# Deformable convolution beside its own set-up: the first batch's places in two halves, and the norm's scales of later batches spread by DMA

## Chip, cores and metric

The kernel runs on one core of a Trainium2 chip. The metric is device time in microseconds for one execution of the whole program; lower is better.

## What is computed

The program is a network of four layers over `x` of 4 batches, 128 channels and 64 x 64 places. Each layer adds a token mixer over a channel norm, and then a feed-forward part. The change lies in the mixer of the second layer, a modulated deformable 3 x 3 convolution. Cut to what matters:

```python
x = x + _L1_conv_ref(_ln_c(x), w_off, b_off, w_mod, b_mod, weight, bias)

def _ln_c(v, eps=1e-6):                     # over the channels of each place
    m = mean(v, axis=1); s = var(v, axis=1)
    return (v - m) / sqrt(s + eps)

def _deform_forward(x, ...):                # K = 3, PAD = 1
    off = conv2d(x, w_off, b_off)           # dy, dx of each place and tap
    mask = sigmoid(conv2d(x, w_mod, b_mod))
    py, px = place + tap + dy, place + tap + dx
    y0, x0 = floor(py), floor(px);  ly, lx = py - y0, px - x0
    # four neighbours, zero outside the image
    sampled = v00*(1-ly)*(1-lx) + v01*(1-ly)*lx + v10*ly*(1-lx) + v11*ly*lx
    return einsum('bckhw,ock->bohw', sampled * mask, weight) + bias
```

## The kernel before

The image stays in SBUF as `xs` (128 channels by 4 batches of 4096 places). The phases run one after another; the deformable stage follows a recurrence and comes before an expert-choice layer.

**The set-up of a batch** is the generator `plan(b)`. Eight chunks of 512 places are centred by a matmul (`centred`), squared on ACT and summed on PE (`deviations`). The root's reciprocal is taken on DVE (`inverted`), in two halves of four chunks. `scaled` spreads one row of the reciprocals over the 128 partitions with a matmul against a broadcast column of the identity, into PSUM, and multiplies the centred chunk by it on DVE (L792, L801). `turned` transposes a chunk by rows and writes it to a table in DRAM, pairs of neighbouring rows side by side (PE L818, ACT L820 and L812, SP L827 and, for the last chunk, L829); its PSUM bank has the tag "pt" (two banks) for batch 0 and "pd" (one bank) for the others, and its SBUF tile `dcn_xt` has two buffers. `offsets` is the small 3 x 3 convolution, four chunks to a call, 36 matmuls, four transposes and four copies into `off` (L840, L849, L853, L858). `places` turns all offsets of the batch, 32 tiles of 128 places by 9 taps, into indices `idx` and weights `w` on DVE and ACT (L915 to L978); L944 writes the indices.

**The main loop** walks over batches, chunks of 512 places (`c`, 8 of them) and 7 of the 9 taps. For each tap it takes four tiles of 128 places in two pairs. `taken` issues two gathers from the table (L998, one indirect DMA a tile, on POOL's queue) into one of eight buffers `dcn_g`, and multiplies them on DVE by their weights, which are held in PSUM (L1006). Two steps later `joined` transposes and adds them on PE (L1015, eight to a pair), then ACT copies (L1120) and `convolve` multiplies by the tap's weights (L1127). The other two taps, the middle column's, are made from hat functions instead of gathers (`hats`, `fold`, L1030 to L1062).

**The order** on PE, ACT, DVE and POOL is the order in which the program is written; SP's DMAs are placed by a scheduler. One `step()` follows each pair: it runs what is due from earlier steps, takes one item of the generator `side` (every fifth step one more), and one item of `hats`. `side` is `plan(b + 1)`. What is left of it at the head of the next batch is drained in one go:

```python
for b in range(B):
    for _ in side:
        pass
    side = plan(b + 1) if b + 1 < B else iter(())
```

`plan(0)` has nothing to run beside and is issued whole ahead of the loop. Its second part sets `turned` of the last four chunks abreast of `offsets(0)`, `offsets(1)` and `places`. `keep` stores `idx` and `w` for a fallback, which is taken only where an offset is over 2.

Of the kernel before, what the change touches and what calls it, by code (L numbers as in the profile page):

```python
# [7 lines left out]

# [2 lines left out]

# [17 lines left out]
P = 128  # L29
# [563 lines left out]
class Sampling:  # L593
# [8 lines left out]
    def __init__(self, net, one, dram):  # L602
# [4 lines left out]
        self.all_idx = [dram.tile([NCH, P, 4 * KK], I32, name=f"dcn_all_idx{b}") for b in range(B)]  # L607
        self.all_w = [dram.tile([NCH, P, 16 * KK], F32, name=f"dcn_all_w{b}") for b in range(B)]
        self.tables = [dram.tile([SIDE * SIDE + 1, 2, P], F32, name=f"dcn_table{b}") for b in range(B)]
        zero = one.tile([SIDE + 1, 2 * P], F32, name="dcn_zero")  # L610
        nc.gpsimd.memset(zero, 0.0)

# [82 lines left out]
def deformable(net, sampling):  # L695
# [19 lines left out]
    with ExitStack() as ctx:  # L715
# [2 lines left out]
        ps = ctx.enter_context(tc.tile_pool(name="dcn_ps", bufs=2, space=PSUM))  # L718
        (xp,) = padded_pair(net, one, PAD, "dcn_pad", 1)
        cw = one.tile([P, NH * P], F32, name="dcn_cw", bufs=1)  # L720
        far = one.tile([P, B + 1], F32, name="dcn_far")
        beyond = one.tile([1, 2], F32, name="dcn_beyond")
        rowts = []
        for i in range(2):
# [11 lines left out]
        def plan(b):  # L736
# [1 line left out]

            def bank(tag="pd" if b else "pt"):
                return ps.tile([P, CH], F32, name=f"dcn_{tag}", tag=tag, bufs=BANKS[tag])

            def inside(c):
# [29 lines left out]
            def inverted(h):  # L774
# [11 lines left out]
                )  # L786
                yield

            def scaled(c):
                rows = slice(32 * (c % 4), 32 * (c % 4) + 32)  # L790
                pb = bank()
                nc.tensor.matmul(  # L792
                    pb,
                    net.ident[rows, rows.start : rows.start + 1].to_broadcast([32, P]),
                    rstds[c // 4][rows],
                    start=True,
                    stop=True,
                )
                yield
                d = inside(c)  # L800
                nc.vector.tensor_mul(d, d, as_shape(pb, d))  # L801
                yield

            xts = []
# [70 lines left out]
                    yield  # L875

            yield from inverted(0)
            for c in half:
                yield from scaled(c)
            if b == 0:  # L880
                yield from abreast(
                    one_by_one(*(turned(c) for c in half)),
                    one_by_one(inverted(1), *(scaled(4 + c) for c in half)),
                )
                yield from abreast(
                    one_by_one(*(turned(4 + c) for c in half)),
                    one_by_one(offsets(0), offsets(1), places(b, off)),
                )
                return
            yield from turned(0)  # L890
            yield from turned(1)
            yield from inverted(1)
            yield from turned(2)
            yield from turned(3)
            for c in half:
                yield from scaled(4 + c)
            yield from offsets(0)
            yield from turned(4)
            yield from turned(5)
            yield from offsets(1)  # L900
            yield from turned(6)
            yield from turned(7)
            yield from places(b, off)

        def places(b, off):

            frac, row = [], new("row")
            hat = sb.tile([P, NT, NH, PICKED], F32, name="dcn_hat", tag="dcn_hat", bufs=1)
            apart = sb.tile([P, NT, NH, 1], F32, name="dcn_apart", tag="dcn_apart", bufs=1)
            pieces = sb.tile([P, NT, NH * PICKED, 3], BF16, name="dcn_pieces", tag="dcn_pieces")  # L910
            at = slice(H0, H0 + NH)
            for axis in range(2):
                pos, low, lowi, over = new("pos"), new("low"), new("lowi", I32), new("over")
                frac.append(new(f"frac{axis}"))
                nc.vector.tensor_add(pos, grids[axis], off[:, :, axis : 18 : 2])  # L915
                if axis == 0:
                    nc.vector.tensor_sub(apart[:, :, :, 0], pos[:, :, at], grids[0][:, :, at])
                    yield
                    nc.vector.tensor_reduce(
                        far[:, b : b + 1],  # L920
                        apart.rearrange("p t k o -> p (t k o)"),
                        AX.X,
                        ALU.max,
                        apply_absolute_value=True,
                    )
# [12 lines left out]
                if axis == 0:  # L938
                    nc.vector.tensor_scalar(row, low, float(SIDE), float(SIDE + 1), op0=ALU.mult, op1=ALU.add)
                else:  # L940
                    nc.vector.tensor_add(row, row, low)
                yield
            idx = new("idx", I32)
            nc.vector.tensor_copy(idx, row)  # L944
            ly, lx = frac
            mask, lo, hi = new("pos"), new("low"), new("over")
            w = new("w")
            wq = [w[:, :, :, q] for q in range(4)]
            nc.scalar.activation(mask, off[:, :, 18:27], AF.Sigmoid)
            yield  # L950
            rows_of = hat[:, :, :, 1:]
            shape = [P, NT, NH, PICKED - 1]
            nc.vector.tensor_tensor(
                rows_of, apart.to_broadcast(shape), sampling.steps[:, :, :, 1:].to_broadcast(shape), ALU.add
            )
            nc.scalar.activation(rows_of, rows_of, AF.Abs)
            yield
            nc.scalar.activation(rows_of, rows_of, AF.Relu, bias=sampling.ones, scale=-1.0)
            nc.vector.tensor_mul(rows_of, rows_of, mask[:, :, at].unsqueeze(3).to_broadcast(shape))
            yield  # L960
            left = hat.rearrange("p t k j -> p t (k j)")
            for a in range(3):
                nc.vector.tensor_copy(pieces[:, :, :, a], left)
                if a < 2:
# [12 lines left out]
            nc.vector.tensor_mul(wq[0], lo, lx)  # L977
            nc.vector.tensor_mul(wq[1], hi, lx)  # L978
            made[b] = (sampling.squares(tables[b]), idx, w, pieces, turns[b])
            yield  # L980

# [121 lines left out]
        with tc.manual_schedule(engines=ORDERED):  # L1103
# [44 lines left out]
            for b in range(B):  # L1148
                for _ in side:
                    pass  # L1150
                side = plan(b + 1) if b + 1 < B else iter(())
                rows, idx, w, pieces, turned = made.pop(b)
                for more in busy:
                    for _ in more:
# [2 lines left out]
                for tile in range(5):  # L1157
                    fold(b, tile, turned)
                for c in range(NCH):
                    nc.vector.tensor_copy(near_w[:, c % 2], w[:, Q4 * c : Q4 * c + Q4])  # L1160
                    po = {}
                    busy.append(hats(b, c, po, pieces, turned))
                    if c == 2:
                        keep(b, idx, w)
                    if b == 0 and c < B:
                        nc.sync.dma_start(sampling.kept[c].rearrange("c p t -> p c t"), as_chunks(net.xs[:, c, :]))
                    for k in BY_ASK:
                        pt = {}
                        for i in range(0, 4, 2):
                            at(2, joined, pt, i, taken(rows, idx, c, k, i))  # L1170
                            if i:
                                at(4, turn_back, k, pt, po, b, c)
                            step()
            while later:
                step()
            nc.vector.tensor_reduce(far[:, B : B + 1], far[:, 0:B], AX.X, ALU.max)
            pt = ps.tile([P, CH], F32, name="dcn_pt", tag="pt", bufs=BANKS["pt"])
            nc.tensor.transpose(pt[0:1, 0:P], far[:, B : B + 1], net.ident)
            nc.vector.tensor_reduce(beyond[:, 0:1], pt[0:1, 0:P], AX.X, ALU.max)
            nc.vector.tensor_scalar(beyond[:, 1:2], beyond[:, 0:1], 2.0, None, op0=ALU.is_gt)  # L1180
            nc.vector.tensor_copy(sampling.flag, beyond[:, 1:2])
# [1470 lines left out]
```

## Time and profile before

| what | value |
|---|---|
| median of three runs | 6021.36 us (6016.81 to 6021.89) |
| the profiled execution | 6020.81 us, span 6018.7 us |
| mean granted TensorE clock | 0.975 |
| busy over the span | PE 94%, DVE 73%, ACT 55%, POOL 34% |
| first and last gather of the stage (L998) | 1313.3 and 2450.4 us, 896 gathers |
| first gather of batches 1, 2, 3 | 1603.0, 1888.6, 2171.6 us |

Times in the profile are microseconds from the span's start. A line of a timeline gives start, duration, engine, source line, operation, output and inputs, and in brackets how long the engine had been idle and what released it. A line of the groups gives a count, then busy time and mean nanoseconds, then idle time ahead and its releasers. PEld is the weight load of TensorE. SPq and POOLq are the issue of DMAs.

### The profile page before, as it was taken

The numbers are of one execution on the slowest core, as the hardware profiler recorded it, in microseconds if no ns is written. First come the engines' busy times: TensorE is split into PE (matmuls) and PEld (weight loads), VectorE is DVE, ScalarE is ACT, GpSimd is POOL, SyncE is SP. The second block draws the span as 40 slices with busy tenths as digits, with TensorE's granted clock in tenths as the row PEclk, the third lists the DMA queues.
The fourth block names the chain that finished last, engine by engine and source line by source line (L and its number), as shares of the span: only waits on it lengthen the run. The fifth ranks groups of instructions, "written<-read, shape, count | busy, mean of one in ns | idle before, by whom it ended". The sixth has DMA issues, their size and how long they took to land. (4 is left out here: it accounts for less than half of the span.)

```text
span 6018.7 us, 97982 instructions
## 1 busy us (share of the span) xinstructions
PE 5660.1 (94%) x39902; PEld 2247.3 (37%) x39933; DVE 4413.8 (73%) x4945; ACT 3332.5 (55%) x4150; POOL 2057.3 (34%) x2015
## 2 busy tenths in 40 slices
PE   8999999889999988879979999999999999999699
PEld 2222222346677666433333222322232223222243
DVE  6888887456667676357446888888888888888687
ACT  4444444332333232431336888888888888899410
POOL 3898897027777777200010111111111111111100
PEclk9999999999999999989989999999999999999899
DMA  6434432047777777550274676656665666666300
GB/s 216 99 73 92 86 78 47 1 142 222 220 231 216 231 220 211 163 203 0 81 266 112 131 158 146 140 127 151 146 144 125 150 146 144 130 136 133 69 25 28
DMA packets 273275, 818.40 MB, mean 136 GB/s; under 512 B 42644, under 2 KB 100392, under 8 KB 226728
## 3 DMA queue, kind: packets, MB, share of 16 engines
q0 software_dynamic: 109568, 505.75, 35.4%
q1 hardware_dynamic: 163240, 306.20, 17.6%
q8 instruction: 320, 5.24, 0.4%
q14 instruction: 147, 1.20, 0.1%
HBM read 416.71 MB, written 93.13 MB: 85 GB/s over the span
## 5 line engine op out<-in xcount | busy, mean ns | idle before, releaser
L2035 ACT ACTIVATE att_ex<-att_sc,att_shift 128x1024 f32<-128x1024 f32 x2048 | 2141.7, 1111 | 282.6 <-PE att_sc L2031 167.7
L2066 DVE TENSOR_TENSOR att_dve<-att_dve,att_ex 128x2048 f32<-128x2048 f32 x704 | 1631.5, 2317 | 155.3 <-ACT att_ex L2035 130.5
L2031 PE MATMUL att_sc<-att_q,att_k 32*128 32x512 f32 x8192 | 1280.9, 640 | 0.5 <-ACT att_ex L2035 0.5
L2047 PE MATMUL att_pv<-att_ex,att_vals 128*32 128x512 f32 x8192 | 1091.9, 605 | 0.0
L998 POOL DMA_INDIRECT dcn_g<-dcn_table,dcn_idx x896 | 851.4, 950 | 354.2 <-issue 151.1
L412 DVE SCALAR_TENSOR_TENSOR inv_prod<-inv_pk,bspan,inv_seen 128x512 f32<-128x512 f32 (+1 forms) x1120 | 774.6, 743 | 140.1 <-PE inv_pk L399 139.8
L410 POOL TENSOR_TENSOR inv_prod<-inv_seen,inv_prod 128x512 f32<-128x512 f32 (+1 forms) x672 | 837.5, 1273 | 94.0 <-ACT inv_prod L409 94.0
L2064 POOL DMA_DIRECT2D att_dma<-att_ex x224 | 192.5, 860 | 1965.4 <-ACT att_ex L2035 1727.4
L409 ACT ACTIVATE inv_prod<-inv_pk,bspan 128x512 f32<-128x512 f32 (+1 forms) x672 | 436.1, 682 | 503.7 <-PE inv_pk L399 493.9
L2031 PEld LDWEIGHTS att_sc<-att_q,att_k 32*128 32x128 f32 x8192 | 423.0, 183 | 658.4 <-issue 417.1
L1006 DVE TENSOR_TENSOR dcn_g<-dcn_g,dcn_near_w 128x1024 f32<-128x1024 f32 x448 | 539.0, 1214 | 167.9 <-DMA dcn_g<-dcn_table,dcn_idx 151.7
L399 PE MATMUL inv_pk<-inv_red,wtap 32*96 32x512 f32 (+1 forms) x3584 | 511.4, 636 | 7.3 <-DVE wtap L377 7.3
L1015 PE MATMUL dcn_pt<-ident,dcn_g 128*128 128x128 f32 x3584 | 473.1, 276 | 37.5 <-ACT dcn_st L1120 12.6
L1015 PEld LDWEIGHTS dcn_pt<-ident,dcn_g 128*128 128x128 f32 x3584 | 418.9, 142 | 210.1 <-issue 122.7
L421 PE MATMUL inv_out<-inv_prod,inv_fold 96*32 96x512 f32 (+1 forms) x3584 | 477.9, 605 | 8.5 <-DVE xs L429 8.5
L2047 PEld LDWEIGHTS att_pv<-att_ex,att_vals 128*32 128x32 f32 x8192 | 161.2, 108 | 752.6 <-issue 727.4
L399 PEld LDWEIGHTS inv_pk<-inv_red,wtap 32*96 32x96 f32 (+1 forms) x3584 | 131.5, 170 | 385.6 <-DVE inv_prod L412 362.1
L1120 ACT COPY dcn_st<-dcn_pt 128x512 f32<-128x512 f32 x224 | 129.9, 580 | 241.2 <-PE dcn_pt L1015 241.2
L1034 ACT ACTIVATE dcn_fold<-dcn_pf,dcn_turn 128x256 f32<-128x256 f32 x128 | 60.2, 473 | 365.1 <-PE dcn_pf L1030 365.1
L1127 PE MATMUL dcn_out<-dcn_st,dcn_wk 128*128 128x512 f32 x448 | 237.4, 612 | 23.3 <-DVE xs L1135 21.4
L2554 PE MATMUL top_po<-top_xg,top_cwe 128*128 128x512 f32 x512 | 233.7, 597 | 0.0
L1054 DVE TENSOR_TENSOR dcn_square<-dcn_hx,dcn_by 128x512 f32<-128x512 f32 x192 | 130.1, 678 | 114.2 <-PE dcn_by L1040 75.2
(449 smaller groups left out, 5326.1 us busy)
## 6 DMA issues: line engine op xcount, KB each, us to landing
att_dma<-att_ex POOLq DMA_DIRECT2D x224, 1024.0 KB, 7.0
inv_seen<-inv_image SPq DMA_DIRECT2D x256, 266.0 KB, 9.1
moe_w<-in_L_ffn_weight SPq DMA_DIRECT2D x64, 1024.0 KB, 14.4
att_dma<-att_ex SPq DMA_DIRECT2D x32, 1024.0 KB, 11.2
att_dve<-att_dma POOLq DMA_DIRECT2D x32, 1024.0 KB
moe_table<-moe_xt SPq DMA_DIRECT2D x64, 288.0 KB, 2.8
dcn_table<-dcn_xt SPq DMA_DIRECT2D x32, 512.0 KB, 4.8
dcn_g<-dcn_table,dcn_idx POOLq DMA_INDIRECT x896, 3.7
```

The costliest lines, as they stand in the source:

```text
L399: nc.tensor.matmul(pk[0:m], wtap[half][rg, i, blk], red[rg, h * CH : (h + 1) * CH], start=True, stop=True)
L409: nc.scalar.activation(prod[0:m, h], pk[0:m], AF.Identity, bias=by)
L410: nc.gpsimd.tensor_mul(of, view, of)
L412: nc.vector.scalar_tensor_tensor(out=of, in0=as_shape(pk[0:m], of), scalar=by, in1=view, op0=ALU.add, op1=ALU.mult)
L421: nc.tensor.matmul(po[CR * blk : CR * (blk + 1), h, :], fold[0:m], prod[0:m, h, :], start=unit == 0, stop=unit == UNITS - 1,)
L998: nc.gpsimd.indirect_dma_start(out=g[:, t, :], out_offset=None, in_=rows, in_offset=bass.IndirectOffsetOnAxis(ap=idx[:, Q4 * c + i + t, k ...
L1006: nc.vector.tensor_mul(near, near, by)
L1015: nc.tensor.matmul(pt[0][:, (i + t) * P : (i + t + 1) * P], near[:, t, q, :], net.ident, is_transpose=True, start=i + t + q == 0, stop=i + ...
L2031: nc.tensor.matmul(pes[h // 2][:, h % 2, :], ks[r, t * P : (t + 1) * P], q[r], start=True, stop=True)
L2035: nc.scalar.activation(ex[:, 2 * two : 2 * two + 2, :], pes[two], AF.Exp, bias=shifts[g][:, two : two + 1],)
L2047: nc.tensor.matmul(block["pv"][r], vals[:, t, r], ex[:, h, :], start=t == 0, stop=t == NT - 1)
L2066: nc.vector.tensor_add(block[who], block[who], ex)
```

## The change

It has two parts. For batch 0, `places` works on a part of the tiles: `plan(0)` ends after `offsets(0)` and the places of the first 16 tiles (chunks 0 to 3), and `offsets(1)` with the places of the other 16 goes into `rest`, which runs as side work ahead of `plan(1)` and is finished by the head of chunk 3 at the latest. For batches 1 to 3, `scaled` no longer uses a matmul: `spread_out` writes four rows of reciprocals to DRAM, and one DMA for each chunk reads a row back into all 128 partitions (`way`, 256 KB); `inverted(1)` moves ahead of the first `scaled`, and the order of `turned` and `scaled` is shifted. `far` gets a column more, and `keep` moves from chunk 2 to chunk 4.

```diff
-            def bank(tag="pd" if b else "pt"):
+            front = [b == 0]
+
+            def bank(tag=None):
+                tag = tag or ("pt" if front[0] else "pd")
                 return ps.tile([P, CH], F32, name=f"dcn_{tag}", tag=tag, bufs=BANKS[tag])
...
+            ways = {}
+
+            def spread_out(h):
+                nc.sync.dma_start(sampling.spread[b][4 * h : 4 * h + 4, :], rstds[h][0:P:32])
+                yield
+                for c in range(4 * h, 4 * h + 2):
+                    way(c)
+                    yield
+
+            def way(c):
+                by = ways[c] = sb.tile([P, CH], F32, name="dcn_way", tag="ln_sq", bufs=4)
+                nc.sync.dma_start(by, sampling.spread[b][c : c + 1, :].to_broadcast([P, CH]))
+
             def scaled(c):
-                rows = slice(32 * (c % 4), 32 * (c % 4) + 32)
-                pb = bank()
-                nc.tensor.matmul(
...
+                if b:
+                    pb = ways.pop(c)
+                else:
+                    rows = slice(32 * (c % 4), 32 * (c % 4) + 32)
+                    pb = bank()
+                    nc.tensor.matmul(
...
                 yield
                 d = inside(c)
                 nc.vector.tensor_mul(d, d, as_shape(pb, d))
+                if b and c % 4 < 2:
+                    way(c + 2)
                 yield
...
             yield from inverted(0)
-            for c in half:
-                yield from scaled(c)
             if b == 0:
+                for c in half:
+                    yield from scaled(c)
                 yield from abreast(
                     one_by_one(*(turned(c) for c in half)),
                     one_by_one(inverted(1), *(scaled(4 + c) for c in half)),
                 )
+                held = places_held(b)
                 yield from abreast(
                     one_by_one(*(turned(4 + c) for c in half)),
-                    one_by_one(offsets(0), offsets(1), places(b, off)),
+                    one_by_one(offsets(0), places(b, off, held, slice(0, NT // 2), 0)),
                 )
+                front[0] = False
+                rest.append(one_by_one(offsets(1), places(b, off, held, slice(NT // 2, NT), B)))
                 return
+            yield from spread_out(0)
+            yield from inverted(1)
+            for c in half:
+                yield from scaled(c)
+            yield from spread_out(1)
             yield from turned(0)
             yield from turned(1)
-            yield from inverted(1)
+            for c in half:
+                yield from scaled(4 + c)
             yield from turned(2)
             yield from turned(3)
-            for c in half:
-                yield from scaled(4 + c)
             yield from offsets(0)
             yield from turned(4)
             yield from turned(5)
             yield from offsets(1)
             yield from turned(6)
             yield from turned(7)
-            yield from places(b, off)
+            yield from places(b, off, places_held(b), slice(0, NT), b)
...
-                side = plan(b + 1) if b + 1 < B else iter(())
+                side = chain(rest[0] if b == 0 else (), plan(b + 1) if b + 1 < B else ())
...
                 for c in range(NCH):
+                    if b == 0 and c == NCH // 2 - 1:
+                        for _ in rest[0]:
+                            pass
...
-                    if c == 2:
+                    if c == NCH // 2:
                         keep(b, idx, w)
```

Inside `places` every tile is cut to the part's columns (`off[:, part]`, `grids[axis][:, part]` and so on); its operations are the same, once for each part.

More of the change, by code (lines that the diff above doesn't have):

```diff
@@ L10 @@
 from functools import partial
+from itertools import chain
 import concourse.bass as bass
@@ L609, in __init__ @@
         self.tables = [dram.tile([SIDE * SIDE + 1, 2, P], F32, name=f"dcn_table{b}") for b in range(B)]
+        self.spread = [dram.tile([NCH, CH], F32, name=f"dcn_spread{b}") for b in range(B)]
         zero = one.tile([SIDE + 1, 2 * P], F32, name="dcn_zero")
@@ L720, in deformable @@
         cw = one.tile([P, NH * P], F32, name="dcn_cw", bufs=1)
-        far = one.tile([P, B + 1], F32, name="dcn_far")
+        far = one.tile([P, B + 2], F32, name="dcn_far")
         beyond = one.tile([1, 2], F32, name="dcn_beyond")
@@ L787, in inverted @@
                 yield
-            def scaled(c):
-                rows = slice(32 * (c % 4), 32 * (c % 4) + 32)
-                pb = bank()
[L792 to L798, printed above, removed]
+            ways = {}
[8 more added lines that the diff above has]
+                nc.sync.dma_start(by, sampling.spread[b][c : c + 1, :].to_broadcast([P, CH]))
+            def scaled(c):
+                if b:
[4 more added lines that the diff above has]
+                    nc.tensor.matmul(
+                        pb,
+                        net.ident[rows, rows.start : rows.start + 1].to_broadcast([32, P]),
+                        rstds[c // 4][rows],
+                        start=True,
+                        stop=True,
+                    )
                 yield
@@ L902, in plan, with places_held @@
             yield from turned(7)
-            yield from places(b, off)
-        def places(b, off):
-            frac, row = [], new("row")
+            yield from places(b, off, places_held(b), slice(0, NT), b)
+        rest = []
+        def places_held(b):
             hat = sb.tile([P, NT, NH, PICKED], F32, name="dcn_hat", tag="dcn_hat", bufs=1)
@@ L910, in places, with some @@
             pieces = sb.tile([P, NT, NH * PICKED, 3], BF16, name="dcn_pieces", tag="dcn_pieces")
+            idx, w = new("idx", I32), new("w")
+            return hat, apart, pieces, idx, w
+        def places(b, off, held, part, column):
+            n = part.stop - part.start
+            def some(name, dtype=F32):
+                return new(name, dtype)[:, part]
+            off = off[:, part]
+            hat, apart, pieces, idx, w = (t[:, part] for t in held)
+            spots = [grid[:, part] for grid in grids]
+            frac, row = [], some("row")
             at = slice(H0, H0 + NH)
             for axis in range(2):
-                pos, low, lowi, over = new("pos"), new("low"), new("lowi", I32), new("over")
-                frac.append(new(f"frac{axis}"))
-                nc.vector.tensor_add(pos, grids[axis], off[:, :, axis : 18 : 2])
+                pos, low, lowi, over = some("pos"), some("low"), some("lowi", I32), some("over")
+                frac.append(some(f"frac{axis}"))
+                nc.vector.tensor_add(pos, spots[axis], off[:, :, axis : 18 : 2])
                 if axis == 0:
-                    nc.vector.tensor_sub(apart[:, :, :, 0], pos[:, :, at], grids[0][:, :, at])
+                    nc.vector.tensor_sub(apart[:, :, :, 0], pos[:, :, at], spots[0][:, :, at])
                     yield
                     nc.vector.tensor_reduce(
-                        far[:, b : b + 1],
+                        far[:, column : column + 1],
                         apart.rearrange("p t k o -> p (t k o)"),
@@ L942, in places @@
                 yield
-            idx = new("idx", I32)
             nc.vector.tensor_copy(idx, row)
             ly, lx = frac
-            mask, lo, hi = new("pos"), new("low"), new("over")
-            w = new("w")
+            mask, lo, hi = some("pos"), some("low"), some("over")
             wq = [w[:, :, :, q] for q in range(4)]
@@ L951, in places @@
             rows_of = hat[:, :, :, 1:]
-            shape = [P, NT, NH, PICKED - 1]
+            shape = [P, n, NH, PICKED - 1]
             nc.vector.tensor_tensor(
@@ L978, in places @@
             nc.vector.tensor_mul(wq[1], hi, lx)
+            _, _, pieces, idx, w = held
             made[b] = (sampling.squares(tables[b]), idx, w, pieces, turns[b])
@@ L1175, in deformable @@
                 step()
-            nc.vector.tensor_reduce(far[:, B : B + 1], far[:, 0:B], AX.X, ALU.max)
+            nc.vector.tensor_reduce(far[:, B + 1 :], far[:, 0 : B + 1], AX.X, ALU.max)
             pt = ps.tile([P, CH], F32, name="dcn_pt", tag="pt", bufs=BANKS["pt"])
-            nc.tensor.transpose(pt[0:1, 0:P], far[:, B : B + 1], net.ident)
+            nc.tensor.transpose(pt[0:1, 0:P], far[:, B + 1 :], net.ident)
             nc.vector.tensor_reduce(beyond[:, 0:1], pt[0:1, 0:P], AX.X, ALU.max)
```

## Prediction

> **What bounds the kernel now.** I read the page's slices first: POOL is busy in one early stretch only, so its 34% of the span says little. That stretch is the deformable stage, and the table by stretches shows it (columns: length, then busy time and instruction count of PE, PEld, DVE, ACT, POOL, then granted clock, DMA share, GB/s):
> ```profile
> core 0: us, PE busy (x) PEld busy (x) DVE busy (x) ACT busy (x) POOL busy (x), PEclk, DMA share, GB/s
> 2000.00:2100.00 100.00, 97.07 (x671) 64.66 (x672) 58.88 (x67) 28.54 (x54) 75.52 (x80) 1.00 0.78 232
> 2300.00:2400.00 100.00, 85.53 (x553) 67.35 (x554) 60.95 (x62) 25.46 (x47) 75.63 (x81) 0.95 0.72 211
> ```
> PE looks like the limit at 97%, but when the last batch takes the side work away and PE falls to 85.5%, POOL still does 80 to 81 gathers in 100 us. The timeline of POOL says why:
> ```profile
> 1313.32 1.26 POOL L998 DMA_INDIRECT dcn_g<-dcn_table,dcn_idx  x1 [67.58 <-DVE dcn_idx L944]
> ...
> 1533.23 0.95 POOL L998 DMA_INDIRECT dcn_g<-dcn_table,dcn_idx  x1 [1.75 <-DVE dcn_g L1006]
> ...
> 1601.78 0.95 POOL L998 DMA_INDIRECT dcn_g<-dcn_table,dcn_idx  x1 [0.30 <-DMA dcn_g<-dcn_table,dcn_idx]
> 1603.03 0.95 POOL L998 DMA_INDIRECT dcn_g<-dcn_table,dcn_idx  x1 [0.30 <-issue]
> ```
> A gather takes 0.95 us and 0.30 us pass before the next, whatever the row names as releaser: one per 1.25 us. 895 intervals of 1.25 are 1118.8 us; from 1313.32 to the last gather at 2450.39 are 1137.1. So POOL sets the stage but for 18.3 us, and it starts only when `dcn_idx` is there (67.58 us idle). The last two rows are the change from batch 0 to batch 1: no hole.
>
> Of the 18.3 us, by batch 9.7, 5.5, 2.9 and 0, some 13.4 (7.0, 4.3, 2.1) are waits like the one at 1533: all eight `g` buffers are full because PE is behind. How far behind I read per pair, from the start of its second gather to its first transpose:
> ```profile
> 1518.83 0.94 POOL L998 DMA_INDIRECT dcn_g<-dcn_table,dcn_idx  x1 [0.30 <-issue]
> 1539.82 1.04 PE L1015 MATMUL dcn_pt<-ident,dcn_g 128*128 128x128 f32 x8
> ```
> That is pair 80 of batch 0: 21 us, the worst. The same distance is 6.5 to 11 us at pairs 0 to 44, 12.8 at the last pair, 5.1 in most of batch 3, where nothing is at the side. POOL stops from about 18.
>
> **Part 1, the start.** The timeline of all engines around the first gather:
> ```profile
> 1294.30 0.80 DVE L858 COPY dcn_off<-dcn_pt 128x108 f32<-128x108 f32 x4 [16.52 <-PE dcn_pt L853]
> 1298.38 0.62 SPq L829 DMA_DIRECT2D dcn_table<-dcn_xt  x1
> 1304.76 0.80 DVE L858 COPY dcn_off<-dcn_pt 128x108 f32<-128x108 f32 x4 [9.66 <-PE dcn_pt L853]
> 1305.59 0.46 DVE L915 TENSOR_TENSOR dcn_pos<-dcn_at,dcn_off 128x288 f32<-128x288 f32 x1
> 1312.71 0.31 DVE L944 CAST dcn_idx<-dcn_row 128x288 int32<-128x288 f32 x1
> ```
> Half the offsets are in place at 1295.1; the gather waits for the other half and for twenty DVE instructions, 1305.59 to 1313.02, 7.4 us. With 144 columns in place of 288, nine of 0.46 us should fall to some 0.31 and eight of 0.31 to 0.23 (an estimate: these rows have about 0.16 us that doesn't shrink), in all 5.4 us: indices at 1300.5. Then the table is late next. Its last large write is issued at 1297.75 and lands 4.5 us on. The last group of transposes no longer queues behind 1.9 us of `offsets(1)` matmuls, but its bank is held until the copy at 1294.30 ends, so it gains some 1.2 us, part of which the write ahead of it (packets until 1298.1) takes back. First gather at 1301.8 for 1313.3: **−11.5 us** (−10.5 to −12.5).
>
> `offsets(1)` and the second half of the places now run beside the gathers: 36 matmuls at 0.11 and four transposes, 4.8 us of PE, and some 4 us of fixed DVE time for the doubled instructions. Both cost nothing while POOL sets the pace; the cover is the backlog, which has 9 us of room at the start of batch 0. Past that they would cost what they take.
>
> **Part 2, the hole between batch 0 and 1.** This is the price, and it is counted from the code. A batch has 112 steps, each takes one item of the side line and every fifth a second: 112 + 22 = 134. `plan(1)` had 123 items (centred 16, deviations 4, inverted 12, scaled 16, turned 32, offsets 24, places 19), so it ended 11 items early. Now `rest` comes first with 31 (12 and 19) and `spread_out` adds 6: 160. The 26 left are drained at once at the head of batch 1, and the built order shows it: behind the last gather of batch 0 come all of `places(1)` on DVE, and on PE the four transpose groups of `turned(6)` and `turned(7)`, ahead of the transposes of the last pair. No gather of batch 1 can start before.
>
> Let the last gather of batch 0 start at T. The transposes of the pair before it (second gather at T − 2.5) begin one backlog later. For the backlog I add up the zones of the trace: `offsets` raised it by about 4 us each time (batch 2: 10 to 14, 14.6 to 18.6), `scaled` by 3 to 7, `turned` left it or lowered it by up to 3. `scaled` has left PE, so from 7 us, two `offsets` and a `turned` between them give 7 + 4 − 2 + 4 = 13. The transposes then end at T + 11.6. Four groups follow with one bank of tag "pd": 0.6 on PE, 0.58 for the ACT copy L820, 0.2 between, 1.4 each, T + 17.2. The write is issued and lands 4.8 us later (median of L827): first gather at T + 22.1 where it was T + 1.25. **+20.8 us.** The indices are no later: last multiplication T + 9.4, then 7.4 us. With the 5 us backlog of batch 3 the hole is 12.8, with the 21 of pair 80 it is 28.8. At the two later ends 129 items meet 134, so no hole.
>
> **Part 3, the scales by DMA.** In batches 1 to 3 it removes these PE rows and the waits of DVE for them:
> ```profile
> L792 PE MATMUL dcn_pd<-ln_rstd,ident 32*128 32x512 f32 x48 | 27.7, 658 | 0.0
> L801 DVE TENSOR_TENSOR dcn_pad<-dcn_pad,dcn_pd 128x512 f32<-128x512 f32 x24 | 16.5, 686 | 37.8 <-PE dcn_pd L792 37.8
> ```
> 27.7 us, 9.2 a batch, and none on the path by itself. What it buys is the room that PE lacks: with 9.2 us less the peaks of 20.7 and 18.6 stay under 18, and in batch 0 the heavy zones now come last. Of the 13.4 us of full-buffer stalls I take **−12** (−5 to −13.4).
>
> It adds 6 spread writes and 24 reads of 256 KB on SP, 0.32 us of issue each by the like `att_by` rows, which land in 6.2 us (3.6 to 6.8). The first read is asked ten items, 21 us, ahead of its multiplication, and in SP's built order all four of a half go out without waiting for the half before them to be multiplied, save the second four. So DVE should not wait; if it did, the gathers' multiplications L1006 are queued behind it, and one landing per half, 6 x 6.2 us, would go into the backlog first. SP is also moved: the table writes of batches 1 to 3 now stand behind the eight reads, and ACT's `xt` copies wait for them (9.8 us over 4 waits today); the third comes about 10 us after the last read is free to go, against 4.8 for the landing. Nothing on the path. `keep` at chunk 4 has no one waiting.
>
> One thing speaks against it. A gather starting under a DVE product of two SBUF tiles can be longer:
> ```profile
> 1321.56 0.68 DVE L978 TENSOR_TENSOR dcn_w<-dcn_over,dcn_frac 128x288 f32<-128x288 f32 x1
> 1321.67 1.26 POOL L998 DMA_INDIRECT dcn_g<-dcn_table,dcn_idx  x1 [0.30 <-issue]
> ```
> 1.26 for 0.95. Under L801, whose second input is in PSUM, none of 29 was. After the change both of its inputs are in SBUF. Over the products of that kind in `places` the excess is 0 to 0.15 us on the mean, some 0.065: 24 times that is **+1.6** (0 to 24 x 0.31 = 7.4).
>
> [...]
>
> **Sum.** −11.5 + 20.8 − 12 + 1.6 = −1.1 us. The profiled execution took 6020.81 (span 6018.7), the median is 6021.36: 6019.7 by the one, 6020.3 by the other. I say 6020.
>
> **Rivals.** *Slower:* the backlog at the last pair of batch 0 is near its old peak, 18 to 21, since the two `offsets` zones now stand back to back with the end. Hole 26 to 29, and then full buffers remain as well (−6): −11.5 + 27.5 − 6 + 3 = +13, 6034. For it: those zones made the peak. Against: `scaled`, the other half of the climb, is gone from PE. It decides from about 18. *Faster:* PE keeps up as in batch 3, backlog 5, hole 12.8, no stalls: −12.5 − 13.4 + 12.8 = −13, 6008. For it: 9.2 us of PE less; against: `offsets` fills PE even so. *No early start:* the first gathers still wait for all of `dcn_idx`, 0 in place of −11.5: 6031. The built order shows the second half's index write free of any wait for POOL, which speaks against it.
>
> **How the numbers follow.** About 0.2%, 12 us, is what a measurement of this kernel can tell from no change. Forecast 0.61, no early start 0.03 (its 6031 is still within 12 us), slower rival 0.20, faster rival 0.14, and 0.02 for a delay that I don't name. Within 0.2%: 0.64; faster 0.14; slower 0.22. The bounds together give −13 to +21 (6008 to 6041); the upper corner needs every term at its end, so I stop at the slower rival: 6008 to 6034.
>
> **What would show it.** First gather near 1302; a hole of about 21 us on POOL some 281 us later, with the release by the table write; batches 1 and 2 of 281 us each for 285.6 and 283.0; L801's successor waiting for no DMA. Wrong if there is no hole, if the gathers' 1.25 us changes, or if time moves outside this stage.

## The result, and the profile after

| | kernel before | changed kernel |
|---|---|---|
| median of 20 runs each | 6023.52 us (6014.80 to 6031.12) | 6031.00 us (6024.69 to 6038.11) |
| ratio, 95% interval | | 1.0014 [1.0008, 1.0021] |
| profiled execution, span | 6020.81, 6018.7 us | 6031.23, 6029.3 us |
| first gather of batches 0 to 3 | 1313.3, 1603.0, 1888.6, 2171.6 | 1299.8, 1608.0, 1891.6, 2176.3 |

The changed kernel is **7.5 us slower** (interval 4.8 to 12.6). That is within the forecast range and under the 0.2% named there, but the sign is the opposite of the −1.1 us that was added up.

The table by stretches of the changed kernel, at the same two places as before:
```profile
core 0: us, PE busy (x) PEld busy (x) DVE busy (x) ACT busy (x) POOL busy (x), PEclk, DMA share, GB/s
2000.00:2100.00 100.00, 93.85 (x664) 67.33 (x666) 61.90 (x70) 31.59 (x62) 75.63 (x81) 1.00 0.80 242
2300.00:2400.00 100.00, 87.34 (x561) 68.61 (x564) 60.68 (x62) 25.45 (x47) 75.63 (x80) 0.95 0.73 210
```
TensorE fell from 97 to 94 in the full stretch, and GpSimd still does 80 to 81 gathers in 100 us. The pace is what it was. The timeline of GpSimd shows what moved, at the start and between batch 0 and batch 1:
```profile
1299.84 1.23 POOL L1041 DMA_INDIRECT dcn_g<-dcn_table,dcn_idx  x1 [59.32 <-DVE dcn_pieces L1005]
...
1580.85 0.95 POOL L1041 DMA_INDIRECT dcn_g<-dcn_table,dcn_idx  x1 [0.30 <-issue]
1608.03 0.95 POOL L1041 DMA_INDIRECT dcn_g<-dcn_table,dcn_idx  x1 [26.23 <-PE dcn_pf L1073]
1609.28 0.94 POOL L1041 DMA_INDIRECT dcn_g<-dcn_table,dcn_idx  x1 [0.30 <-issue]
```
The first gather comes earlier, and behind the last gather of batch 0 there is now a hole: 27.18 us from start to start where 1.25 is the pace, so 25.9 us. The releaser named, the fold matmul L1073, is not the cause. The timeline of all engines shows what ended last:
```profile
1578.35 0.95 POOL L1041 DMA_INDIRECT dcn_g<-dcn_table,dcn_idx  x1 [0.31 <-issue]
...
1594.00 0.80 DVE L881 COPY dcn_off<-dcn_pd 128x108 f32<-128x108 f32 x4 [6.47 <-PE dcn_pd L876]
1595.33 1.91 PE L1058 MATMUL dcn_pt<-ident,dcn_g 128*128 128x128 f32 x16
1597.07 0.60 PE L841 MATMUL dcn_pd<-ident,dcn_pad 128*64 128x128 f32 x4
...
1600.93 0.63 PE L841 MATMUL dcn_pd<-ident,dcn_pad 128*64 128x128 f32 x4 [0.67 <-ACT dcn_xt L843]
1602.83 0.64 SPq L852 DMA_DIRECT2D dcn_table<-dcn_xt  x1
1602.96 0.31 DVE L987 CAST dcn_idx<-dcn_row 128x288 int32<-128x288 f32 x1
```
The first row is the second gather of the pair before the last. Its transposes are the second half of the sixteen at 1595.33, so from 1596.3: TensorE is 17.9 us behind. Then come the four transpose groups of the table at 1.3 us each, the last table write at 1602.83, and 5.2 us later the gather. The indices were there at 1603.3.

**The terms.** Single profiles of one kernel differ outside the stage (shown below), so I count the stage alone, from its first `centred` matmul to its last gather, and both kernels were profiled twice. An interval between gathers over 1.25 us is split into its two causes: a gather longer than 0.95 us (lengthened), or a pause longer than 0.30 (a wait).

| us | before, two profiles | changed, two profiles | difference | forecast |
|---|---|---|---|---|
| stage start to first gather (difference at equal variant, see below) | 68.3; 70.9 | 60.0; 60.0 | −10.8 | −11.5 |
| hole | 0; 0 | 25.9; 22.1 | +24.0 | +20.8 |
| waits for full buffers | 14.0; 11.6 | 2.3; 3.6 | −9.8 | −12 |
| gathers lengthened | 4.2; 4.1 | 8.1; 9.6 | +4.7 | +1.6 |
| sum | | | +8.1 | −1.1 |

The front comes in two variants with either kernel. The first offsets are copied 49.3 us after the stage's start, or 51.85 in the profiles where the granted clock was 0.50 all the way from 1260 to 1280. The profile of before in the forecast was of the first kind, its repeat and both of the changed kernel are of the second. The −10.8 is at equal variant: 57.5 (in experiments below) for 68.3, and 60.0 for 70.9. The sum of +8.1 agrees with the +7.5 between the medians.

### The profile page after: what moved, and what is told of

Read it like the earlier page. It is cut to its first block, busy times and chain, and to the rows that moved or that the text cites. A ratio compares the mean times of both kernels' runs of the same rounds, so it can differ in the third digit from the quotient of the medians.

```text
span 6029.3 us, 97989 instructions
## 1 busy us (share of the span) xinstructions
PE 5650.6 (94%) x39854; PEld 2247.9 (37%) x39885; DVE 4420.8 (73%) x4980; ACT 3332.2 (55%) x4153; POOL 2061.4 (34%) x2015
## 3 DMA queue, kind: packets, MB, share of 16 engines
q1 hardware_dynamic: 166744, 312.54, 17.9%
## 5 line engine op out<-in xcount | busy, mean ns | idle before, releaser
L1105 PE MATMUL dcn_out<-dcn_square,dcn_fold 128*128 128x128 f32 x1504 | 205.2, 280 | 0.0
## 6 DMA issues: line engine op xcount, KB each, us to landing
att_dve<-att_dma POOLq DMA_DIRECT2D x32, 1024.0 KB, 10.4
```

## The experiments

Each experiment was timed in five rounds beside the kernel before, except the two repeats, which have one profile each. The same split of the stage gives a sum for each kernel, against the mean of the two profiles of before (waits 12.8, lengthened 4.1). The front is compared at equal variant, but for `kept_later`, whose first offsets come at 49.7 us and which is set against 68.3:

| kernel | front | hole | waits | lengthened | sum | measured, interval |
|---|---|---|---|---|---|---|
| halves_only | −10.7 | +20.5 | −5.1 | −1.1 | +3.6 | +4.9 [−1.8, 9.0] |
| spread_only | 0 | 0 | −8.7 | +3.3 | −5.4 | −2.7 [−7.2, 3.6] |
| both_paced | −10.8 | 0 | −6.7 | +4.1 | −13.4 | −10.9 [−15.0, −4.2] |
| halves_paced | −10.7 | 0 | +7.8 | −1.1 | −4.0 | −4.2 [−9.0, 1.8] |
| few_taps | −10.8 | +17.8 | −12.8 | +3.1 | −2.7 | +0.1 [−6.6, 4.2] |
| third | −10.8 | +11.1 | −3.9 | +2.7 | −0.9 | +4.0 [−1.8, 9.0] |
| product_in_sbuf | 0 | 0 | −1.5 | +5.1 | +3.6 | +2.1 [−4.8, 6.0] |
| kept_later | −10.4 | 0 | −5.3 | +3.0 | −12.7 | −12.4 [−19.3, −7.8] |

Every sum lies inside its measured interval. The intervals are some ten us wide, so the terms rest on the profiles, and the times only say that nothing large is missing. Only `both_paced` and `kept_later` can be told from the kernel before.

**The two parts apart.** `halves_only` is the changed kernel with the scales by matmul and the order of steps in `plan` as before; `spread_only` keeps batch 0's front as before:
```diff
 # halves_only, scaled(c), for all batches
-                if b:
-                    pb = ways.pop(c)
+                pb = bank()
+                nc.tensor.matmul(pb, ...)
 # spread_only, plan(0)
-                    one_by_one(offsets(0), places(b, off, held, slice(0, NT // 2), 0)),
+                    one_by_one(offsets(0), offsets(1), places(b, off)),
...
+                rest.append(iter(()))
```


> Only the halves of batch 0; the scales stay a matmul and the old order of batches 1 to 3 stays. Theory (the hole between batch 0 and 1 costs more than the early start brings): first gather 8 to 11 us nearer to the start of the stage; 31 + 123 = 154 items meet 134, so 20 are drained at the head of batch 1, all of the places but no transposes on PE; the hole is then the last multiplication and 7.4 us of DVE up to the indices, 13 to 19 us; full-buffer stalls stay near the 18 us of before. In all 2 to 8 us slower than before, near 6028. Rival (the cost of the change is the DMA spread, its traffic and its SBUF products): no such cost here, so the early start shows in full, 8 to 11 us faster, near 6014.

It has 20 items left at the end of batch 0, and a hole:
```profile
1580.35 0.95 POOL L1034 DMA_INDIRECT dcn_g<-dcn_table,dcn_idx  x1 [0.30 <-issue]
...
1594.42 0.60 PE L836 MATMUL dcn_pd<-ident,dcn_pad 128*64 128x128 f32 x4
...
1595.75 0.31 DVE L980 CAST dcn_idx<-dcn_row 128x288 int32<-128x288 f32 x1
...
1597.19 0.63 SPq L847 DMA_DIRECT2D dcn_table<-dcn_xt  x1
...
1602.11 1.13 POOL L1034 DMA_INDIRECT dcn_g<-dcn_table,dcn_idx  x1 [20.81 <-DVE dcn_hat L1000]
```
21.76 − 1.25 = 20.5, where I had 13 to 19, and the reason that I had given was wrong too: not the indices end last, which were there at 1596.1, but the table. Its last transpose group stands on TensorE at 1594.4, behind the transposes of the last pairs, and its last write was issued at 1597.19, 4.9 us ahead of the gather. So the early start by itself is eaten up by its own hole.

> Only the scales by DMA in batches 1 to 3; batch 0 as before. Theory: 129 items meet 134, no hole at any change of batch; PE has 9.2 us less per batch, so the full-buffer stalls (13.4 us) mostly go; the multiplications by two SBUF tiles lengthen the gathers that they meet by some 4 us in all. 5 to 10 us faster than before, near 6016. Rival (the spread is what costs): 5 to 9 us slower, near 6030, with no hole.

No hole, waits down to 4.1, and a time that can't be told from no change, where I had expected 5 to 10 us faster. In the profile, taking the scales off TensorE did what it was to do, but over a third of it came back as longer gathers.

**Without the hole.** A second item at every second step of batch 0, so that all 160 items fit (112 + 56 = 168), with the whole change and with the halves alone:
```diff
-                if n % 5 == 0:
+                if n % (2 if n <= 14 * NCH else 5) == 0:
                     next(side, None)
```


> The whole change, and in batch 0 every second step takes a second side item in place of every fifth: 112 + 56 = 168 places for 160 items, so nothing is left to drain. Theory: no hole at the head of batch 1 (26 us less than in the changed kernel); the side work is pressed into less time, so some 3 to 8 us of full-buffer stalls come back in batch 0. Early start kept. 10 to 16 us faster than before, near 6011, and some 18 to 22 us faster than the changed kernel. Rival 1 (the hole is only where PE's backlog shows: PE is the real bound of batch 0 and the time comes back as stalls): 20 us or more of stalls in batch 0, time as the changed kernel, near 6030. Rival 2 (the early start is lost to the table writes): as spread_only.

> The halves and the pace of batch 0, the scales by matmul. Theory: no hole, early start kept, but PE has 4.8 us more in batch 0 and none of the relief: stalls of 15 to 22 us in the stage in place of 18. 5 to 10 us faster than before, near 6016; both_paced is 3 to 6 us faster than this. Rival (PE is the bound): 30 us of stalls or more, slower than before.

The timeline of GpSimd in `both_paced`, across the change of batch:
```profile
1583.59 0.95 POOL L1041 DMA_INDIRECT dcn_g<-dcn_table,dcn_idx  x1 [0.31 <-issue]
1584.84 0.95 POOL L1041 DMA_INDIRECT dcn_g<-dcn_table,dcn_idx  x1 [0.30 <-PE dcn_pt L1058]
1586.09 0.95 POOL L1041 DMA_INDIRECT dcn_g<-dcn_table,dcn_idx  x1 [0.30 <-issue]
```
The first gather of batch 1 is the one at 1584.84, 23 us earlier than in the changed kernel. 6008.88 us, ratio 0.9984 [0.9975, 0.9993]: **faster than both kernels**. Only the pacing differs from the changed kernel, so the hole that drained items leave is the price. TensorE is behind here as well: the transposes of the last pair but one start at 1593.1, 12.2 us after its second gather (1580.95), and with nothing left to drain no hole comes of it.

`halves_paced` has no hole either, but its waits are 20.6 us where `both_paced` has 6.1. Of the 7.8 us above before only 3.0 are in batch 0, where the items stand closer; 3.7 are in batch 1 and 1.1 in batch 2. In time, where I had expected 5 to 10 us faster, it can't be told from before, and its interval overlaps that of `both_paced`. On the profiles the pacing pays more with the scales off TensorE; the pacing with the scales by DMA but without the halves was not run.

**Is the hole TensorE's distance, or the drained items?** `few_taps` lightens `offsets` in batches 1 to 3 and leaves the number of items alone:
```diff
-                    for q in range(Q4):
+                    for q in range(Q4 if b == 0 or k in (0, KK - 1) else 0):
```


> The changed kernel, but in batches 1 to 3 the offsets convolution multiplies only two of its nine taps (28 of 36 matmuls of a half left out, about 3.1 us of TensorE per half; the number of items is unchanged, and these batches' offsets are not the reference's). Theory: the hole between batch 0 and 1 is the backlog of TensorE at the last pair (17.9 us in the changed kernel's profile) plus about 8 us for the last transposes and the table write, so with lighter offsets the backlog falls to 11 to 14 us, the hole from 25.9 to 19 to 22, and the full buffers cost less as well: 6 to 10 us faster than the changed kernel, about 0 beside the kernel before. Rival: the hole is set by the 26 items drained at once, not by the backlog: hole 24 to 27, within 3 us of the changed kernel, some 5 to 8 above the kernel before.

Its timeline has the same rows as that of the changed kernel above:
```profile
1577.71 0.95 POOL L1041 DMA_INDIRECT dcn_g<-dcn_table,dcn_idx  x1 [0.30 <-issue]
...
1580.21 0.95 POOL L1041 DMA_INDIRECT dcn_g<-dcn_table,dcn_idx  x1 [0.30 <-issue]
...
1586.53 1.91 PE L1058 MATMUL dcn_pt<-ident,dcn_g 128*128 128x128 f32 x16
...
1599.27 0.94 POOL L1041 DMA_INDIRECT dcn_g<-dcn_table,dcn_idx  x1 [18.11 <-PE dcn_pf L1073]
```
Distance 1587.5 − 1577.7 = 9.8 us, hole 19.06 − 1.25 = 17.8. The same 26 items are drained, and the hole is 8.1 us shorter with a distance 8.1 us shorter than in the first profile of the changed kernel. Both had a mean granted clock of 0.96 from 1300 to 1596, so it is not the clock that makes this difference. Beside the second profile (13.9 and 22.1, below) they are shorter by 4.1 and 4.3. The rival, that the number of items alone sets the hole, falls. That items are left to drain stays the condition for one, as `both_paced` shows.

**Fewer items left.** `third` gives a second item at every third step of batch 0 (112 + 37 = 149 of 160):
```diff
-                if n % 5 == 0:
+                if n % (3 if n <= 14 * NCH else 5) == 0:
```


> The changed kernel with a second side item at every third step of batch 0 in place of every fifth: 112 + 37 = 149 of 160 items fit, 11 are drained at once, all of them of the second half of places(1); the transposes and the table write are done before. Theory: the hole falls to between 8 and 14 us (DVE's own distance of about 9 us behind the last gather, then the last index instructions), the full buffers of batch 0 cost 5 to 8 in place of 2.2; in all 7 to 13 us faster than the changed kernel, 0 to 6 faster than the kernel before. Rival: TensorE's distance at the last pair grows as the items come closer together, and the hole stays above 18: no more than 4 us faster than the changed kernel.

```profile
1583.32 0.62 SPq L852 DMA_DIRECT2D dcn_table<-dcn_xt  x1
...
1586.50 0.95 POOL L1041 DMA_INDIRECT dcn_g<-dcn_table,dcn_idx  x1 [0.30 <-issue]
...
1597.81 0.31 DVE L987 CAST dcn_idx<-dcn_row 128x288 int32<-128x288 f32 x1
1598.86 0.94 POOL L1041 DMA_INDIRECT dcn_g<-dcn_table,dcn_idx  x1 [11.41 <-DVE dcn_hat L995]
```
With only places left, the indices set the hole and not the table, whose last write went out 15.5 us ahead of the gather: 11.1 us, as expected. The expected time was not met: +4.0 us beside the kernel before, where I had 0 to 6 faster. Beside the +7.5 of the changed kernel that is 3.5 us, which is what the rival gave (no more than 4), though its reason, a hole above 18, did not come. Its stage is 1.9 us shorter than that of before in the first profiles, and its interval reaches to −1.8, so the runs do not decide whether anything is missing there.

**The scale product by itself.** In the kernel before, the scale goes from PSUM to SBUF over ScalarE, so that L801 has two SBUF inputs, with no new DMA:
```diff
+                if b:
+                    by = sb.tile([P, CH], F32, name="dcn_way", tag="ln_sq", bufs=4)
+                    nc.scalar.copy(by, pb)
+                    pb = by
                 d = inside(c)
                 nc.vector.tensor_mul(d, d, as_shape(pb, d))
```


> The kernel before, where in batches 1 to 3 ScalarE copies the spread scale from PSUM to SBUF and VectorE multiplies two SBUF tiles (24 copies of some 0.58 us; matmuls and everything else as before, no new DMA). Theory: gathers that meet this product grow by some 0.14 us each on the mean, 4 to 5 us over all in the gathers' own durations, where the kernel before shows 0.0; the time 2 to 6 us above the kernel before, part of it absorbed where POOL waits for buffers anyway. Rival: in the changed kernel it was the spread reads of 256 KB that slowed the gathers, not the product: gathers under the product unchanged at 0.95, time within 2 us of the kernel before.

First its product and a gather under it, then the same in the changed kernel:
```profile
1443.16 0.69 DVE L805 TENSOR_TENSOR dcn_pad<-dcn_pad,dcn_way 128x512 f32<-128x512 f32 x1
1443.28 1.38 POOL L1002 DMA_INDIRECT dcn_g<-dcn_table,dcn_idx  x1 [0.31 <-DVE dcn_g L1010]
```
```profile
1454.56 0.68 DVE L822 TENSOR_TENSOR dcn_pad<-dcn_pad,dcn_way 128x512 f32<-128x512 f32 x1
1454.64 1.43 POOL L1041 DMA_INDIRECT dcn_g<-dcn_table,dcn_idx  x1 [0.30 <-issue]
```
28 gathers meet the product in `product_in_sbuf` and are longer by 0.175 us on the mean, 0.52 at most, 4.9 us in all. In the changed kernel it is 31 by 0.144 and, in the second profile, 28 by 0.198; under L801 of before, 29 and 30 by 0.0. All of it falls on gathers that start while the product runs (18 of the 31, by 0.25 us); the 13 that were already running are not longer. So the product is enough to explain the longer gathers, and little is left for the reads of 256 KB. The time, +2.1 us, can't be told from no change.

On the mean a gather under the product lost 0.144 to 0.198 us, 0.21 to 0.29 of the product's 0.69 us, and never the whole of it (0.52 at most). How the product slows it no run shows.

**Is the table's landing shortened without other writes?** The four writes of the kept activations move into the loop, with the pacing of `both_paced`:
```diff
-                        nc.sync.dma_start(sampling.kept[c]...)
+                        nc.scalar.dma_start(sampling.kept[c]...)
```


> The kernel with batch 0's items paced closer (every second step two), and the four writes of the kept activations issued by ScalarE's queue inside the first four chunks in place of SyncE's at the start of the stage. Theory: the first gather waits for the table's last write, whose packets share the DMA engines with these writes; without them the first gather comes 2 to 5 us earlier (53 to 55.5 us behind the stage's start for 57.5), the stage ends as much earlier, 13 to 16 us below the kernel before. Rival: the write's landing of about 5 us is its own latency: first gather at 57 to 58, time as without this edit, 9 to 12 below the kernel before; and the writes in the loop may cost the gathers bandwidth, some us more.

```profile
1292.42 0.64 SPq L852 DMA_DIRECT2D dcn_table<-dcn_xt  x1
...
1297.74 1.23 POOL L1041 DMA_INDIRECT dcn_g<-dcn_table,dcn_idx  x1 [57.14 <-DVE dcn_hat L1001]
```
First gather 57.9 us behind the stage's start, 5.3 us after the last table write (1292.42 to 1297.74), as in `both_paced` (1293.47 to 1298.83, 5.4 us). The four writes are out of the way here: the first is issued at 1300.45, and the DMA share from 1240 to 1260 is 0.00 for 0.85. The rival was right, the landing does not come from these writes. The time, 6008.07 us, ratio 0.9978 [0.9968, 0.9987], beats both kernels as well and can't be told from `both_paced`.

**Both kernels once more.**

> The kernel before once more, unchanged, for a second profile. From the first centred matmul of the deformable stage to the last gather it took 1205.4 us, and 3568.3 us from there to the end. If single profiles differ outside the stage by chance, this one gives a stage within 3 us of 1205 and a remainder anywhere from 3568 to 3578, as the other kernels show. Rival: the change lengthens what follows the stage; then the remainder is again within 1 us of 3568.

Stage 1205.3 us for 1205.4, remainder 3579.8 for 3568.3: the same kernel differs by 11.5 us outside the stage. That is why the profiles' spans are not compared here.

> The changed kernel once more, unchanged. By the theory of the hole: 24 to 28 us between the last gather of batch 0 and the first of batch 1, the distance of TensorE at the last pair 16 to 20 us, gathers under the two-SBUF product longer by 0.12 to 0.17 us; the first gather 57.5 us behind the stage's start if TensorE is granted its clock there, 60 if it is granted half of it as in the first profile.

```profile
1579.61 0.95 POOL L1041 DMA_INDIRECT dcn_g<-dcn_table,dcn_idx  x1 [0.30 <-issue]
...
1582.12 0.94 POOL L1041 DMA_INDIRECT dcn_g<-dcn_table,dcn_idx  x1 [0.30 <-issue]
...
1592.54 1.91 PE L1058 MATMUL dcn_pt<-ident,dcn_g 128*128 128x128 f32 x16
...
1605.50 1.06 POOL L1041 DMA_INDIRECT dcn_g<-dcn_table,dcn_idx  x1 [22.44 <-DVE dcn_pieces L1005]
```
Distance 1593.5 − 1579.6 = 13.9, hole 22.1, both below what I expected. With 17.9 and 25.9, and 9.8 and 17.8 in `few_taps`, three profiles lie on one line: **the hole is the distance and 8.0 to 8.2 us**. In `halves_only`, where one transpose group of the table is behind the last pairs in place of four, it is the distance of 15.7 and 4.8.

The two profiles of the changed kernel part at about 1494 us. TensorE's rows there, first profile and then second:
```profile
1494.11 1.09 PE L1058 MATMUL dcn_pt<-ident,dcn_g 128*128 128x128 f32 x8 [2.00 <-DVE dcn_g L1049]
1495.89 1.89 PE L1058 MATMUL dcn_pt<-ident,dcn_g 128*128 128x128 f32 x8 [0.47 <-ACT dcn_st L1163]
1498.83 2.08 PE L1170 MATMUL dcn_out<-dcn_st,dcn_wk 128*128 128x512 f32 x2 [0.62 <-DVE xs L1178]
```
```profile
1497.65 1.12 PE L1170 MATMUL dcn_out<-dcn_st,dcn_wk 128*128 128x512 f32 x2 [1.42 <-DVE xs L1178]
```
The windows at the same place, first profile and then second:
```profile
1490.00:1500.00 10.00, 6.86 (x31) 4.47 (x31) 7.16 (x10) 1.34 (x3) 7.68 (x8) 0.80 0.77 250
1500.00:1510.00 10.00, 10.00 (x70) 8.68 (x69) 8.49 (x10) 1.36 (x3) 7.56 (x9) 0.86 0.71 198
```
```profile
1490.00:1500.00 10.00, 8.45 (x53) 6.09 (x53) 8.45 (x11) 3.23 (x7) 7.87 (x8) 1.00 0.74 231
1500.00:1510.00 10.00, 10.00 (x78) 8.86 (x78) 7.08 (x8) 2.52 (x6) 7.57 (x9) 1.00 0.69 204
```
In the first profile TensorE had a pause of 2.00 us, the clock fell (0.80 and 0.86 of full in the two windows), and eight transposes took 1.9 us in place of 1.04. In the second a pause of 1.42 us left the clock at 1.00. The length of the pause does not tell the two apart, for in the kernel before the clock fell behind one of 1.42 us, to 0.57 in the window after it:
```profile
1866.38 1.27 PE L1015 MATMUL dcn_pt<-ident,dcn_g 128*128 128x128 f32 x8 [1.42 <-issue]
```
```profile
1867.00:1871.00 4.00, 4.00 (x17) 2.68 (x15) 3.93 (x7) 1.78 (x3) 3.01 (x3) 0.57 0.73 207
```
The distance was 5.6 us in both profiles at pair 60, and at pair 80 11.4 in the first and 6.7 in the second; some 4 us of that difference stayed up to the hole. The lost clock in the two windows is 20% and 14% of ten us, 3.4 us, but it does not account for all of it: the second profile had lost more just before (0.66 from 1460 to 1470, the first 0.83), so that from 1458 to 1512 the clock was 0.91 in the first and 0.94 in the second, some 1.6 us apart, and 1.4 us of the difference is that the second profile's gathers came later. I read this from the rows and did not test it by a kernel; what set the two apart stays open in part.

## Why the prediction was wrong

**The start was right.** −10.8 for −11.5. As forecast the table is late next: the indices come at 1297.65, the last write is issued at 1294.47, the gather follows at 1299.84.
```profile
1291.66 0.80 DVE L881 COPY dcn_off<-dcn_pt 128x108 f32<-128x108 f32 x4 [15.52 <-PE dcn_pt L876]
1294.47 0.64 SPq L852 DMA_DIRECT2D dcn_table<-dcn_xt  x1
1297.65 0.23 DVE L987 CAST dcn_idx<-dcn_row 128x144 int32<-128x144 f32 x1
```

**The hole was right in its mechanism and too small.** What is late, in which order, and the four groups were as forecast. Counted from the last gather of batch 0, the transposes end at +16.2 and, in the second profile, +12.2 (forecast +11.6), the groups take 5.1 and 5.5 us (5.6), the last large write and its landing 5.9 and 5.7 (4.8). The term of the hole that failed is the distance of 13: 17.9 and 13.9 measured. Within its sum 7 + 4 − 2 + 4, the zones held: in the second profile 6.7 at pair 80, +4.3 over the first `offsets`, −1.6 over `turned`, +4.4 over the second to the last pair. The starting 7 did not always hold. It was 11.4 in the first profile, where the clock fell shortly before (to 0.50 from 1498 to 1502); a fall of the clock is not in that sum. The rest of the hole's error is the landing.

**The stalls were too hopeful.** Of the full-buffer waits 9.8 us went, for −12. The 13.4 that I started from was one profile; its repeat has 11.6 by the split used here, for 14.0. Waits did not end in batches 1 and 2 (0.7 to 2.3 each), and with 2.8 to 3.0 of longer gathers these two take 283.6 to 285.1 us each, not 281.

**The longer gathers were under-sized threefold,** +4.7 for +1.6, inside the bound of 7.4. I took the mean over all two-SBUF products in `places`, most of them shorter than 0.69 us. The twelve of 0.68 to 0.70 us that run beside gathers in the trace of before (L974, L977, L978) lengthen them by 0.15 us a product, and 24 times that would have been +3.7. DVE waits for no DMA on the ways, as forecast:
```profile
L822 DVE TENSOR_TENSOR dcn_pad<-dcn_pad,dcn_way 128x512 f32<-128x512 f32 x24 | 16.4, 684 | 0.0
```

Hole +3.2, waits +2.2, longer gathers +3.1 and start +0.7 make the 9.2 us between −1.1 and +8.1. All four erred to the hopeful side. Each alone would have left the forecast within 0.1% of no change; together they gave it the wrong sign. The two profiles share the error out differently: the hole is 5.1 and 1.3 us over its forecast, the waits 1.5 and 2.8, the longer gathers 2.3 and 3.9. So the steps that failed are sizes: the distance at the last pair, the stalls that would go, and the price of the second SBUF input. What waits for what was as forecast.

**The rivals.** The slower rival named the right mechanism, with distance 18 and hole 26 in the first profile. But full buffers did not remain at −6, and the result lies between it and the forecast. The faster rival's distance of 5 was never seen, though the `few_taps` kernel came to 9.8; 5.1 is near the floor of batch 3 in the trace of before, where the median is 6.1 and the highest 9.8. No time moved outside the stage that repeats of one kernel do not show as well, and the early start was real.

## What to carry to other kernels

When work is put ahead of a side line that has just enough slots, count the slots: 26 items too many cost more than the 11 us that the early start won, and one line of pacing gave them back. What is drained at a batch's end waits behind the whole backlog of the engine that it needs, so the price is that engine's distance there plus the chain to the next start (17.9 and 8.0 us here), while a backlog of 12.2 us with nothing to drain left no hole, and the distance has to be read from more than one profile. A product moved from PSUM to SBUF to relieve one engine can slow another through its second input (0.144 and 0.198 us a gather here); price it by rows of the same size.

## What the hardware showed that I had not expected

- A 0.69 us DVE product with two SBUF inputs lengthened a gather that met it by 0.10 to 0.20 us on the mean of each of eight profiles, and 0.52 at most; in the first profile of the changed kernel all of it fell on the 18 of 31 that started under it, 0.25 us each on the mean. With the second input in PSUM it was 0.0 in 59 cases.
- A pause of 2.00 us on TensorE was followed by a granted clock of 0.50 for the four us from 1498, and some 4 us by which its distance then differed from the second profile's were still there at the hole, some 95 us later. A pause of 1.42 us in the kernel before also preceded a fall, to 0.57 over the four us from 1867, while another of 1.42 us, in the second profile of the changed kernel, did not (1.00 from 1498 to 1502).
- Outside the stage, one kernel's two profiles differed by 11.5 us, more than the whole effect.
